# Layer norm's squares added on GpSimd before TensorE sums them, in a two-layer image kernel

## The chip, the cores and the metric

The kernel runs on one core of a Trainium2 chip. The metric is the device time of one execution in microseconds (us). The core's engines work side by side, each through its own queue and in the order of that queue: TensorE (PE in the profile, PEld for its weight loads), VectorE (DVE), ScalarE (ACT), GpSimd (POOL), and SyncE (SP), which here only issues DMAs.

## What is computed

Eight images of 384 channels and 64 x 64 pixels pass two residual layers. The first layer is a group norm, a layer norm over the channels, and attention in windows of 8 x 8 pixels: one half of the heads (branch 0) on plain windows, the other half (branch 1) on windows shifted by 4 pixels. The second is a group norm, a channel mixing, a filter in the frequencies of each 8 x 8 block, a 3 x 3 convolution of each channel, a gate and a second mixing. The change touches the variance of the layer norm alone:

```python
x = x + _L0_conv_ref(_gn(x), ...)          # layer 0
x = x + _L1_conv_ref(_gn(x), ...)          # layer 1

# in _L0_conv_ref
xt = x.reshape(b, c, h * w).transpose(0, 2, 1)
mu = xt.mean(-1, keepdims=True)
var = ((xt - mu) ** 2).mean(-1, keepdims=True)
xt = (xt - mu) / jnp.sqrt(var + EPS) * norm_g + norm_b
qkv = (xt @ qkv_w + qkv_b).reshape(b, h * w, 3, c).transpose(2, 0, 1, 3)
...
out = out @ proj_w + proj_b
```

## The kernel before

**Tiles.** An image is cut into 8 strips of 8 rows, 512 pixels each, so there are 64 strips. A strip is a tile of 128 partitions x 3 chunks of channels x 512 pixels in float32 (384 channels = 128 x 3), with the pixels put in the order of the windows.

**A strip's way through layer norm.** `group_normal` (L308, VectorE) writes the group-normed strip y. `ln_square` (L313, ScalarE) squares all three chunks into `sq`, of which there is one buffer. `ln_sums` (L317 on) lets TensorE sum y and `sq` over the channels: a matrix of ones scaled by 1/384, 32 columns wide, is the weight, and for each of the three chunks four matmuls of 128 pixels write to four groups of 32 rows of one PSUM bank (`ln`). These are 12 matmuls for y and 12 for `sq`; each float32 matmul is two records in the profile. ScalarE copies the sums out (`m`, L325), VectorE and ScalarE form one over the standard deviation (`lr`, L327 to L330), and two DMAs spread it over all partitions by way of DRAM (`line`, `rs`). `ln_scale` (L341, VectorE) multiplies y by it. The mean is not subtracted from y: the weights were centred for that.

**What follows.** `shifted_half` (L354 to L356, POOL) copies halves of two neighbouring strips into `y2` (and `yw`) for branch 1. `qk_tile` (pq) and `v_tile` (pvv) are the projections on TensorE, `scores` (pS), `weights` and `exponent` the softmax, `turn` (pT) and `apply` (pA) the weighted sum, `put` (po) and `project` (pr) the output. `v_tile` also has POOL set a column of ones in `v` (L397). In the second layer `mix` (pt), `transform` (pf), `back` (pz), the convolution (`conv`, L651, up to eight VectorE instructions a chunk, on the accumulator zz) and `finish` (pw on TensorE, the output sum x_finish on VectorE, L684) follow.

**The order.** All pieces are put in a list with a due place each and emitted sorted by it; a unit of place is half of a strip's share of time. The attention of one image runs beside the second layer of the image before it, so the first image has attention alone and the last second layer stands alone at the end. `ln_square` has its place at v + 0.45 and `ln_sums` at v + 0.99, where v is two strips ahead of the strip's attention. A scheduler may reorder what is emitted, but for the TensorE instructions, which keep the order of the program.

**The start.** Before the first attention the kernel reads the first image, takes its group statistics, and prepares the weights: `pack_qk` (L118) gathers the q and k columns on VectorE and POOL, and `qk_weights` and `v_weights` fold the norm's bias in (`pb`, `pv`) and centre the weights (`pc` on TensorE, then a subtraction on VectorE, L185). In TensorE's order the first strip's `ln_sums` stands ahead of all of this preparation, the second strip's behind the first `pc`. On POOL the 64 small DMAs of the position tables (`rpb_raw`, L154) and the memsets of the convolution's borders (L268, L269) come first, then POOL's part of `pack_qk`.

Of the kernel before, what the change touches and what calls it, by code (L numbers as in the profile page):

```python
# [9 lines left out]
ALU = mybir.AluOpType  # L10
AX = mybir.AxisListType

P = 128
KC = 3
# [18 lines left out]
def block_kernel(ctx: ExitStack, tc: tile.TileContext, out, x, consts, fsel, wqk, wv, bqk, bv,  # L33
                 wp, bp, lng, lnb, rpb1, rpb2, w_in, w_dw, w_out, filt):
    nc = tc.nc
# [8 lines left out]
    def psum(name):  # L44
        return ps.tile([P, ST], F32, tag="gemm", name=name)
# [6 lines left out]
    def matmul(*args, **kw):  # L52
        tc.keep_in_program_order(nc.tensor.matmul(*args, **kw))  # L53
# [4 lines left out]
    def strip(tag, bufs, name):  # L58
        return sb.tile([P, KC, ST], F32, tag=tag, bufs=bufs, name=name)

    def row512(tag, bufs, name):
        return sb.tile([P, ST], F32, tag=tag, bufs=bufs, name=name)
# [9 lines left out]
    for s in range(NS):  # L72
        tag, bufs = ("x", 5) if s < 5 else (("xn", 1), ("ow", 1), ("y2", 1))[s - 5]
        t = strip(tag, bufs, f"x_first{s}")
# [188 lines left out]
    xs, ys, y2s, qks, vs, os_, ots, x1s, zs = ({} for _ in range(9))  # L263
# [47 lines left out]
    def ln_square(b, s):  # L311
        sq = ys[b, s, "sq"] = strip("sq", 1, f"sq_{b}_{s}")
        nc.scalar.activation(sq, ys[b, s], AF.Square)  # L313

    def ln_sums(b, s):


        p = psum(f"ln_{b}_{s}")
        for to, t in ((0, ys[b, s]), (P, ys.pop((b, s, "sq")))):
            for k in range(KC):  # L320
                for j in range(4):
                    matmul(p[32 * j:32 * (j + 1), to:to + P], ones_c[:, 0:32], t[:, k, j * P:(j + 1) * P],
                           start=(k == 0), stop=(k == KC - 1))
        m = sb.tile([P, 2 * P], F32, tag="lc", bufs=1, name=f"m_{b}_{s}")
        nc.scalar.copy(m, p[:, 0:2 * P])  # L325
        rc = sb.tile([P, P], F32, tag="lr", bufs=2, name=f"lr_{b}_{s}")
        nc.vector.tensor_tensor(rc, m[:, 0:P], m[:, 0:P], ALU.mult)  # L327
        nc.vector.tensor_tensor(rc, m[:, P:2 * P], rc, ALU.subtract)
        nc.scalar.activation(rc, rc, AF.Sqrt, bias=eps_t)
        nc.vector.reciprocal(rc, rc)  # L330

        line = dr.tile([4, P], F32, tag="line", bufs=4, name=f"line_{b}_{s}")
        queue = nc.scalar if b == 0 and s < 2 else nc.sync
        queue.dma_start(out=line, in_=rc[0:P:32, :])
        rs = ys[b, s, "rs"] = row512("rs", 2, f"rs_{b}_{s}")
        queue.dma_start(out=rs, in_=bass.AP(line.tensor, line.offset, [[0, P], [1, ST]]))
# [354 lines left out]
    for b in range(B):  # L691
# [17 lines left out]
        for s in range(NS):  # L709
# [3 lines left out]
            at(v - 0.84, load, b, s, "norm")  # L713
            at(v + 0.15, group_normal, b, s)
            at(v + 0.45, ln_square, b, s)
            at(v + 0.99, ln_sums, b, s)
            at(v + 1.35, ln_scale, b, s)

# [163 lines left out]
```

## Time and profile before

| | |
|---|---|
| Time, median of 3 runs | 3784.95 us (3780.62 to 3785.55) |
| The profiled execution | 3783.99 us, of which span 3782.0 |
| TensorE busy | 3675.0 us (97%) |
| VectorE busy | 2819.9 us (75%) |
| ScalarE busy | 2379.1 us (63%) |
| GpSimd busy | 272.9 us (7%) |
| Sums of y (`ln<-y`), 1536 records | 56.6 us busy |
| Sums of squares (`ln<-sq`), 1536 records | 54.5 us busy |
| Squares (L313), 64 instructions | 95.1 us busy, 1486 ns each |

The span is the part of an execution that the trace covers, from its first instruction to its last. Busy time counts each moment once, however many records overlap in it; that is why 1536 matmuls of some 275 ns make 55 us. A share of busy time is an average over stages with different limits: what a change is worth is read from the stage it lies in, by what is waited for there. The profile names tiles without their numbers and lines by `kernel.py`; all matmuls are recorded at L53, all transposes at L56, so TensorE's work is told apart by the tile that it writes.

### The profile page before, as it was taken

To read this page: it belongs to the slowest core of one execution; us is meant where nothing else is said; L and a number is where in the kernel's file an instruction comes from. 1 tells how busy PE (TensorE), PEld (TensorE's weight loads), DVE (VectorE), ACT (ScalarE), POOL (GpSimd) and SP (SyncE) were. 2 spreads that over 40 slices of the span, in tenths; PEclk is the share of its full clock that TensorE was granted. 3 is DMA by queue.
4 is the path that set the end of the run, shared out by engine and by line. 5 is a ranking of instruction groups with operands and counts; after the bars stand their busy time and mean duration, and the time that the engine had idled before them with its cause. 6 is when DMAs were issued, how large, how long until landed. Compare 5 with 4: busy or idle time off the path is not lost.

```text
span 3782.0 us, 90249 instructions
## 1 busy us (share of the span) xinstructions
PE 3675.0 (97%) x39168; PEld 2347.3 (62%) x39168; DVE 2819.9 (75%) x4601; ACT 2379.1 (63%) x3946; POOL 272.9 (7%) x648
## 2 busy tenths in 40 slices
PE   6999999999999999999999999999999999999998
PEld 4666666666666666665666666666666666666554
DVE  5655578778878688777877778877788777777898
ACT  3766676656666576665766666666676666676442
POOL 4000000000000000000000000000000000000000
PEclk9999999999999999999999999999999999999999
DMA  4222223223322233223332322322232222222422
GB/s 121 88 96 85 89 85 111 82 87 123 117 91 104 74 120 119 103 80 115 115 104 93 109 91 99 132 79 107 93 119 99 107 88 82 98 79 74 157 101 76
DMA packets 144496, 377.16 MB, mean 100 GB/s; under 512 B 12308, under 2 KB 12900, under 8 KB 144100
## 3 DMA queue, kind: packets, MB, share of 16 engines
q1 hardware_dynamic: 139952, 370.60, 27.8%
q8 instruction: 308, 5.05, 0.6%
q0 software_dynamic: 2048, 0.15, 0.1%
q10 hardware_dynamic: 2100, 0.63, 0.1%
q14 instruction: 88, 0.72, 0.1%
HBM read 270.54 MB, written 100.79 MB: 98 GB/s over the span
## 4 chain that ended last, share of the span: by engine, by line
PE 87%; DVE 5%; ACT 4%; DMA 2%; issue 2%; SPq 0%; ACTq 0%; DVEq 0%
PE pq L53 24%; PE pt L53 13%; PE pr L53 13%; PE pvv L53 12%; PE pw L53 7%; PE pS L53 3%; PE pA L53 3%; PE pz L53 3%; PE pT L56 3%; PE po L56 3%; PE ln L53 2%; DVE zz L651 2%; PE pf L53 2%; PE pc L53 1%; DMA rs<-line 1%
## 5 line engine op out<-in xcount | busy, mean ns | idle before, releaser
L651 DVE SCALAR_TENSOR_TENSOR zz<-z,dw_sb,zz 128x512 f32<-128x512 f32 x1490 | 1089.9, 750 | 192.6 <-ACT zz L645 169.7
L53 PE MATMUL pq<-y,wqk_sb 128*128 128x512 f32 x2160 | 990.1, 596 | 0.0
L53 PEld LDWEIGHTS pq<-y,wqk_sb 128*128 128x128 f32 x2160 | 402.8, 190 | 456.2 <-issue 423.3
L53 PE MATMUL pt<-wi_sb,xn 128*128 128x384 f32 x1536 | 535.2, 487 | 1.4 <-DVE x_finish L684 1.4
L53 PE MATMUL pr<-oT,wp_sb 128*128 128x512 f32 x1152 | 523.1, 593 | 1.0 <-DVE oT L515 1.0
L53 PE MATMUL pvv<-wv_sb,y 128*128 128x192 f32 x2880 | 495.9, 326 | 0.0
L53 PEld LDWEIGHTS pvv<-wv_sb,y 128*128 128x128 f32 x2880 | 471.7, 190 | 36.2 <-issue 23.0
L372 ACT ACTIVATE qab<-pq,bq_sb,cst 96x512 f32<-96x512 f32 (+1 forms) x256 | 197.8, 773 | 400.0 <-PE pq L53 398.3
L53 PEld LDWEIGHTS pt<-wi_sb,xn 128*128 128x128 f32 x1536 | 286.2, 190 | 206.8 <-issue 48.0
L372 ACT ACTIVATE kcd<-pq,vec 32x512 f32<-32x512 f32 x512 | 348.4, 680 | 9.0
L53 PEld LDWEIGHTS pr<-oT,wp_sb 128*128 128x128 f32 x1152 | 211.2, 190 | 224.3 <-issue 211.8
L327 DVE TENSOR_TENSOR lr<-m 128x128 f32<-128x128 f32 x64 | 18.7, 292 | 355.4 <-ACT m L325 355.4
L645 ACT ACTIVATE zz<-z,dw_sb 128x512 f32<-128x512 f32 x183 | 133.9, 733 | 199.8 <-PE pw L53 195.2
L372 ACT ACTIVATE qcd<-pq,bq_sb,cst 96x512 f32<-96x512 f32 (+1 forms) x256 | 197.0, 769 | 43.9 <-PE pq L53 40.6
L524 DVE SCALAR_TENSOR_TENSOR x_add<-pr,vec,x_add 128x512 f32<-128x512 f32 x192 | 143.5, 747 | 108.5 <-PE pr L53 106.5
L354 POOL COPY y<-y 128x384 f32<-128x384 f32 x112 | 99.7, 890 | 1719.7 <-PE pvv L53 1217.1
L562 ACT COPY t<-pt 128x384 f32<-128x384 f32 x256 | 124.7, 487 | 157.4 <-PE pt L53 154.3
L406 ACT COPY v<-pvv 128x384 f32<-128x384 f32 x256 | 121.6, 479 | 142.2 <-PE pvv L53 141.5
L53 PE MATMUL pw<-zz,wo_sb 128*128 128x512 f32 x384 | 182.9, 613 | 0.0
L372 ACT ACTIVATE kab<-pq,vec 96x512 f32<-96x512 f32 (+1 forms) x256 | 174.1, 680 | 8.8 <-PE pq L53 7.1
L56 PEld LDWEIGHTS pT<-cst,e 128*128 128x128 f32 x1024 | 119.3, 141 | 66.9 <-issue 40.1
L441 DVE TENSOR_TENSOR e<-e,mx 128x1024 f32<-128x1024 f32 x128 | 158.0, 1234 | 2.5
(138 smaller groups left out, 5194.9 us busy)
## 6 DMA issues: line engine op xcount, KB each, us to landing
x_add<-in_x_dram SPq DMA_DIRECT2D x64, 768.0 KB, 9.4
x1d<-x_add SPq DMA_DIRECT2D x64, 768.0 KB, 5.4
x_mix<-x1d SPq DMA_DIRECT2D x64, 768.0 KB, 4.3
x_finish<-x1d SPq DMA_DIRECT2D x64, 768.0 KB, 6.4
out_dram<-x_finish SPq DMA_DIRECT2D x64, 768.0 KB, 3.8
x_norm<-in_x_dram SPq DMA_DIRECT2D x61, 768.0 KB, 7.7
x_stats<-in_x_dram SPq DMA_DIRECT2D x56, 768.0 KB, 8.0
rs<-line SPq DMA_DIRECT2D x62, 256.0 KB, 3.3
```

Of the source, the lines that this page charges most:

```text
L53: tc.keep_in_program_order(nc.tensor.matmul(*args, **kw))
L56: tc.keep_in_program_order(nc.tensor.transpose(*args, **kw))
L327: nc.vector.tensor_tensor(rc, m[:, 0:P], m[:, 0:P], ALU.mult)
L354: nc.gpsimd.tensor_copy(dst[:, :, :, :, 0:4], src[:, :, :, :, 4:8])
L372: return nc.scalar.activation(dst[to:to + n], pq[of:of + n], AF.Identity, bias=bias[of:of + n], scale=scale)
L406: nc.scalar.copy(v[:, 2 * g:2 * g + 2, :, 0:HD], pvv[:, 0:384].rearrange("p (g h d) -> p g h d", g=2, h=4))
L441: zs["soft"] = nc.vector.tensor_tensor(e, e, mx.unsqueeze(2).to_broadcast([P, 2 * NS, 64]), ALU.subtract)
L524: nc.vector.scalar_tensor_tensor(t[:, m, :], pr, bp_sb[:, m:m + 1], t[:, m, :], ALU.add, ALU.add)
L562: nc.scalar.copy(t1, pt[:, 0:C])
L645: nc.scalar.activation(zz.rearrange("p (r c) -> p r c", c=SW), z[:, 1:9, 1:SW + 1], AF.Copy, scale=dw_sb[:, m, 4:5])
L651: i = nc.vector.scalar_tensor_tensor(acc.rearrange("p (r c) -> p r c", c=SW), z[:, dy:dy + 8, dx:dx + SW], dw_sb[:, m, TAPS[tap]:TAPS[tap] ...
```

## The change

`ln_square` gets two additions on GpSimd, in place: the second and then the third chunk of the squares are added to the first. `ln_sums` sums the three chunks of y as before, but of the squares the first chunk alone. The title under which the change was made also names residuals ahead of the softmax; the code that it means (a dependency called "residual first") is in both kernels, and the diff has nothing of it.

```diff
     def ln_square(b, s):
         sq = ys[b, s, "sq"] = strip("sq", 1, f"sq_{b}_{s}")
         nc.scalar.activation(sq, ys[b, s], AF.Square)
+        for k in (1, 2):
+            nc.gpsimd.tensor_tensor(sq[:, 0, :], sq[:, 0, :], sq[:, k, :], ALU.add)
 
     def ln_sums(b, s):
 
 
         p = psum(f"ln_{b}_{s}")
-        for to, t in ((0, ys[b, s]), (P, ys.pop((b, s, "sq")))):
-            for k in range(KC):
+        for to, t, n in ((0, ys[b, s], KC), (P, ys.pop((b, s, "sq")), 1)):
+            for k in range(n):
                 for j in range(4):
                     matmul(p[32 * j:32 * (j + 1), to:to + P], ones_c[:, 0:32], t[:, k, j * P:(j + 1) * P],
-                           start=(k == 0), stop=(k == KC - 1))
+                           start=(k == 0), stop=(k == n - 1))
```

## The prediction

> **What bounds the kernel now.** I read the page first: the shares of busy time, then the chain that ended last. Its lines give span or busy microseconds with the share of the span.
>
> ```profile
> PE 3675.0 (97%) x39168; PEld 2347.3 (62%) x39168; DVE 2819.9 (75%) x4601; ACT 2379.1 (63%) x3946; POOL 272.9 (7%) x648
> PE 87%; DVE 5%; ACT 4%; DMA 2%; issue 2%; SPq 0%; ACTq 0%; DVEq 0%
> ```
>
> TensorE holds the chain for 87% and is busy 97%. Cut into stretches, it is busy 26.1 of the first 61 us and 3313.5 of the 3359 us from 61 to 3420, where all other layer norms lie: there it is idle 45 us, in pieces of at most 2.7 us. So in that long stretch a microsecond taken from TensorE is a microsecond off the end. The first 61 us are another regime: a serial chain. The second look was therefore the timeline around one layer norm (start, duration, engine, line, operands):
>
> ```profile
> 581.12 1.48 ACT L313 ACTIVATE sq<-y 128x1536 f32<-128x1536 f32 x1 [2.06 <-DVE y L308]
> 583.56 0.12 POOL L397 MEMSET v<- 128x16 f32 x1 [15.94 <-ACT z L607]
> 610.64 0.86 PE L53 MATMUL ln<-y,cst 128*32 128x128 f32 x24
> 611.32 0.84 PE L53 MATMUL ln<-sq,cst 128*32 128x128 f32 x24
> 612.08 0.88 PE L53 MATMUL pf<-t,cst 64*64 64x192 f32 x16
> ```
>
> Twelve matmuls show as 24 records (two for each float32 matmul). The 24 sums of y occupy TensorE from 610.64 to 611.32, 0.68 us, 28.3 ns a record: four column groups run side by side, so the 273 ns of one record is not its price. The square is finished at 582.60, and TensorE wants it 28.7 us later. Over the 64 strips that slack is 14 to 45 us, but for the first two, where it is 0.05 and 1.74 us. So the third look was the chain and POOL's timeline at the start:
>
> ```profile
> 34.55 1.49 ACT sq L313
> 36.09 1.51 PE ln L53 x24
> 37.60 3.93 PE pb L53 x18
> 41.53 4.05 PE pc L53 x6
> 60.94 7.72 PE pq L53 x18
> ...
> 40.95 5.81 POOL L154 DMA_DIRECT2D rpb_raw<-in_rpb_dram  x10 [0.46 <-DMA rpb_raw<-in_rpb_dram]
> 47.22 0.49 POOL L269 MEMSET z<- 128x10 f32 x1
> 47.26 2.00 POOL L118 COPY wqk_sb<-wqk_raw 128x48 f32<-128x48 f32 x6
> ```
>
> From 36.09 TensorE goes through the weight preparation with 1.5 us of idle time to the first pq at 60.94. The first sum of squares stands at the head of that run. POOL meanwhile issues 64 small DMAs one by one until 46.8, and clears borders until 47.5.
>
> **What the Trainium skill says.** Three places bear on this.
> - "GPSIMD Engine Reference", section Elementwise — side-by-side cycle accounting: a two-input add of 2048 float32 a partition takes 4497 ns; a quarter of that is 1.12 us for 512. No run before shows such an add; POOL's one-input copy of 384 takes 0.50 us alone, 0.67 us for 512 if scaled.
> - The same page, section Instruction dispatch: the first call of a freshly loaded GpSimd library pays about 6 us more, with no instruction to show for it. No run here shows it.
> - "SBUF — State Buffer", section Who interferes with whom: a VectorE instruction with two SBUF inputs and a GpSimd instruction that reads SBUF exclude each other for a whole instruction. The trace agrees in kind: the 0.50 us copy L354 takes 1.43 where it meets a subtraction with two SBUF inputs, and the 0.74 us convolution tap behind it takes 0.99.
>
> ```profile
> 565.01 1.22 DVE L441 TENSOR_TENSOR e<-e,mx 128x1024 f32<-128x1024 f32 x1
> 565.15 1.43 POOL L354 COPY y<-y 128x384 f32<-128x384 f32 x1 [7.85 <-DVE y L341]
> 566.14 0.99 DVE L651 SCALAR_TENSOR_TENSOR zz<-z,dw_sb,zz 128x512 f32<-128x512 f32 x1
> ```
>
> **The change part by part.** The built order of instructions shows what the diff alone does not. On TensorE 512 matmuls (8 a strip) are gone and the rest stands as it was. POOL has 128 adds more and, ahead of the first add, one instruction that loads a GpSimd library. VectorE and ScalarE are reordered in the first 60 us only; the SP queue and its DMAs are the same. That the change doesn't do what it says is thus excluded.
>
> *TensorE.* 16 records fewer a strip, at 28.3 ns: 0.453 us. Times 62 strips with slack: **-28.1 us**. If the whole interval of the group (611.32 to 612.08, 0.76 us) shrank in proportion, it were 0.51 us and 31.6; if the last matmul's tail or the next group's inputs ate a little, 0.40 and 25. The first two strips run at 63 and some 41 ns a record: another -1.65, taken with the start.
>
> *The adds in the long stretch.* Two adds, the second waiting for the first, take about 2.4 us against 14 us of slack or more, and from the third strip on POOL's previous instruction ended at least 0.3 us before the square did: TensorE doesn't wait for them. Behind them in POOL's queue stand the memset of v's column of ones (0 to 9 us after the square; read by pA, a phase later) and the copies of the shifted rows, which wait for pvv 20 us on. These cost nothing; if the cover went, pA would be late next, by at most 2.4 us. ScalarE's next square waits for TensorE's read of the single sq buffer, as now.
>
> *VectorE against the adds.* I laid each strip's 2.5 us after the square over VectorE's instructions with two SBUF inputs. They overlap by 26 us in all, in most strips by 0 to 0.25. The exceptions are the fifth strip of each later image (seven, 1.4 to 2.1 us) and the fourth of five of them (1.1 to 1.9), beside two strips at the start. At the fifth, a pair of taps at +1.16 us leads over the output sums to TensorE's pt, which waits for them already:
>
> ```profile
> 932.53 1.54 DVE L651 SCALAR_TENSOR_TENSOR zz<-z,dw_sb,zz 128x512 f32<-128x512 f32 x2 [1.95 <-ACT zz L645]
> 937.41 1.88 DVE L684 TENSOR_TENSOR x_finish<-pw,x_finish 128x512 f32<-128x512 f32 x3
> ```
>
> A pair of 1.12 us adds there holds the taps up by some 1.25 us, of which about 0.6 us of hand-over may hide a half: 0.7 us times 7 images, **+5 us**. Bounds: 0 (a lock can only delay, and VectorE is idle some 23% of the stretch around it), and 15 (1.25 us at all twelve).
>
> *The start.* The first adds stand in POOL's queue behind the 64 DMA issues, the memsets and the library load, and two weight copies stand between them. Borders done 47.5; load 6 (estimate by the skill); add 1.2; two copies 0.7 (their 0.47 and 0.26); add 1.2: 56.6. TensorE's sum of squares starts then and not at 36.1: 20.5 us late, and the whole weight preparation with it, since TensorE takes its queue in order. Less 1.65 for the shorter sums: **+18.9 us** at the first pq, which no idle time behind it takes up (337.5 of 339 us busy from 61 to 400). What else moves there has room. The third strip's adds and the shifted copies behind them on POOL, and on VectorE the second strip's scaling, which now stands ahead of the centring of the second branch's weights, come out at about 86 by the same durations; the second branch's pq, 12.7 us behind the first, needs them at 92. Bounds: no load time and adds of 0.7 give +12; a load of 14 and adds of 2 give +28. Nothing excludes the upper side; a gain is excluded, for POOL is busy until 47.5.
>
> **Sum.** -28.1 + 18.9 + 5 = -4.2. The profiled execution took 3783.99 (span 3782.0 and 2 around it), 1 under the median of 3784.95. 3784.0 - 4.2 gives **3780**.
>
> **The rivals.**
> - *Faster* (chance 0.32): the load costs nothing that shows and VectorE's delays are absorbed. The start then costs 47.5 + 3.1 - 36.1 - 1.65 = 12.9, and -28.1 + 12.9 gives 3769. For it: VectorE idles 0.5 to 2 us after most squares. Against: a library load is in the instructions.
> - *Slower* (0.22): the load in the start takes 20 us, as a fetch from HBM that nothing covers. -28.1 + 32.9 + 5 = +9.8: 3794. It decides from a load of 18 us up. For it: TensorE's whole queue hangs on it. Against: the skill's price is a third of that.
> - *Slower by VectorE* (0.06): the lock is lost in every strip. 2.4 us times 62 is 149; if a sixth of it reached TensorE, +25, and 3784 - 28 + 19 + 25 = 3800. For it: the 1.43 and 0.99 above. Against: 26 us of overlap in all.
>
> **How the numbers follow.** Gain and start nearly cancel in the likeliest case (0.40): within 0.2% (7.6 us, about what a measurement of this kernel can tell from no change), its own range 3776 to 3790. Faster by more 0.32, slower by more 0.28. All low bounds together give 3784 - 31.6 + 12 = 3764, all high ones 3784 - 25 + 28 + 15 = 3802; 3766 to 3797 leaves out the outermost and the lost lock.
>
> **What would show it.** Right: the records of y's sums still 1536, those of sq's 512; from the first pq to the last layer norm the stretch shorter by 23 us (28 less 5); the first sum of squares near 56 to 57 and pq near 80; adds near 1.1 us. Wrong: a first pq before 72 or after 90 (the load), a wait of TensorE for the adds beyond the first two strips, or pt's waits for x_finish grown by over 2 us an image.

## The result, and the profile after

| | before | after |
|---|---|---|
| Time, median of 13 runs | 3783.06 us | 3774.86 us |
| Ratio, 95% interval | | 0.9977 (0.9969 to 0.9986) |
| Profiled execution, its span | 3782.0 us | 3771.3 us |
| First pq of the first image | 60.8 us | 78.3 us |
| Copy of the third strip's sums (m) | 90.8 us | 108.3 us |
| Copy of the last strip's sums (m) | 3404.0 us | 3394.8 us |

The change makes the kernel faster by 0.23% (0.14 to 0.31), 8.7 us. The forecast was 4.2 us, to 3780, and its range of 3766 to 3797 holds the result. Behind the small sum stand two large terms, as forecast: 17.5 us are lost before the first pq, and 26.7 us come back between the third and the last layer norm (3404.0 - 90.8 = 3313.2 us before, 3394.8 - 108.3 = 3286.5 after).

The page of the kernel after: busy time and instructions of each engine, the chain by engine, and the group of the new adds.

```profile
PE 3639.9 (97%) x38144; PEld 2315.5 (61%) x38144; DVE 2839.3 (75%) x4601; ACT 2379.7 (63%) x3946; POOL 438.2 (12%) x776
PE 86%; DVE 5%; ACT 4%; issue 2%; DMA 2%; POOL 0%; ACTq 0%; DVEq 0%; POOLq 0%
L315 POOL TENSOR_TENSOR sq<-sq 128x512 f32<-128x512 f32 x128 | 167.4, 1308 | 634.3 <-ACT sq L313 629.3
```

TensorE has 1024 records fewer and is busy 35 us less, POOL 165 us more, and the chain is still TensorE's. VectorE runs the same 4601 instructions, but they take 19 us more; in the kernel without the adds (below) they take 2819.9 us as before, so it is the adds that lengthen them. An add takes 1.27 us in the median and 1.31 in the mean; the estimate worked out from the Trainium skill's "GPSIMD Engine Reference", section Elementwise — side-by-side cycle accounting, was 1.12.

The timeline of the kernel after around the same strip as in the prediction (start, duration, engine, line, operands):

```profile
594.52 1.49 ACT L313 ACTIVATE sq<-y 128x1536 f32<-128x1536 f32 x1 [2.44 <-DVE y L308]
596.09 2.63 POOL L315 TENSOR_TENSOR sq<-sq 128x512 f32<-128x512 f32 x2 [15.13 <-ACT sq L313]
598.65 0.13 POOL L399 MEMSET v<- 128x16 f32 x1
623.31 0.86 PE L53 MATMUL ln<-y,cst 128*32 128x128 f32 x24
623.99 0.40 PE L53 MATMUL ln<-sq,cst 128*32 128x128 f32 x8
624.33 0.88 PE L53 MATMUL pf<-t,cst 64*64 64x192 f32 x16
```

The adds follow 0.1 us behind the square, are done at 598.7, and TensorE comes for their sum 25 us later. From the first sum of y to pf it now takes 1.02 us instead of 1.44. Over the 62 strips from the third on, the mean from the first sum to TensorE's next group is 1.011 us instead of 1.447: 0.436 us a strip.

The start of the kernel after, in the chain of waits (start, duration, what):

```profile
41.20 6.63 POOL rpb_raw L154 x12
...
48.44 0.03 POOLq L315
48.47 1.30 POOL sq L315
49.78 0.36 POOL wqk_sb L118 x2
50.13 1.23 POOL sq L315
51.36 0.04 issue
51.40 0.66 PE ln L53 x8
52.06 3.93 PE pb L53 x18
...
64.45 1.23 DVE lr L330
65.68 1.42 DVE wv_sb L181
67.10 0.04 issue
67.14 2.93 PE pc L53 x4
70.07 3.65 PE pb L53 x18
```

The chain of the start, which ran over the image's load and TensorE before, runs over POOL's table DMAs now. The library load that the prediction counted on shows only as two records in POOL's queue (MODIFY_POOL_CONFIG, taken here to be the load) at 48.29 and 48.32, 0.15 us each; in the timeline the add begins at 48.39, behind the last memset. TensorE comes to its sum of squares at 51.4, 15.3 us later than before.

### The profile page after: what moved, and what is told of

It reads as the page before. It is cut to its first block, busy times and chain, and to the rows that moved or that the text cites. A ratio compares the mean times of both kernels' runs of the same rounds, so it can differ in the third digit from the quotient of the medians.

```text
span 3771.3 us, 88216 instructions
## 1 busy us (share of the span) xinstructions
PE 3639.9 (97%) x38144; PEld 2315.5 (61%) x38144; DVE 2839.3 (75%) x4601; ACT 2379.7 (63%) x3946; POOL 438.2 (12%) x776
## 4 chain that ended last, share of the span: by engine, by line
PE 86%; DVE 5%; ACT 4%; issue 2%; DMA 2%; POOL 0%; ACTq 0%; DVEq 0%; POOLq 0%
PE pq L53 24%; PE pr L53 13%; PE pt L53 13%; PE pvv L53 12%; PE pw L53 6%; PE pS L53 3%; PE pA L53 3%; PE pz L53 3%; PE pT L56 3%; PE po L56 3%; DVE zz L653 2%; PE pf L53 2%; PE ln L53 2%; PE pc L53 1%; DMA rs<-line 1%
## 5 line engine op out<-in xcount | busy, mean ns | idle before, releaser
L653 DVE SCALAR_TENSOR_TENSOR zz<-z,dw_sb,zz 128x512 f32<-128x512 f32 x1490 | 1106.5, 761 | 189.3 <-ACT zz L647 166.5
L315 POOL TENSOR_TENSOR sq<-sq 128x512 f32<-128x512 f32 x128 | 167.4, 1308 | 634.3 <-ACT sq L313 629.3
L449 ACT ACTIVATE e<-e 128x1024 f32<-128x1024 f32 x128 | 135.3, 1057 | 53.4 <-DVE e L443 52.0
```

The source lines that it names most:

```text
L315: nc.gpsimd.tensor_tensor(sq[:, 0, :], sq[:, 0, :], sq[:, k, :], ALU.add)
L449: nc.scalar.activation(e, e, AF.Exp)
L653: i = nc.vector.scalar_tensor_tensor(acc.rearrange("p (r c) -> p r c", c=SW), z[:, dy:dy + 8, dx:dx + SW], dw_sb[:, m, TAPS[tap]:TAPS[tap] ...
```

## The experiments

All ratios are to the kernel before, which ran beside each of these kernels; "us off" and "us on" are that ratio times its median. The median itself differed between three sessions (3782.4 to 3788.4 us), so kernels are compared by ratio. What is read from a trace is one execution of each kernel.

**The start as before.** In the first three strips neither adds nor shorter sums:

```diff
-        for k in (1, 2):
+        for k in (1, 2) if (b or s > 2) else ():
...
-        for to, t, n in ((0, ys[b, s], KC), (P, ys.pop((b, s, "sq")), 1)):
+        for to, t, n in ((0, ys[b, s], KC), (P, ys.pop((b, s, "sq")), 1 if (b or s > 2) else KC)):
```

> The changed kernel, but the first three strips keep three chunks of squares on TensorE and no adds. Theory (the start pays 17.6 us because the first add stands behind POOL's 64 DMA issues; 0.44 us a strip is gained afterwards): the first pq is back at about 61 us, and 61 strips times 0.44 leave 3783 - 27 = 3756. Rival (the start's loss lies elsewhere, or the steady gain is smaller and the start only looks late): within 5 us of the changed kernel, 3770 to 3780. Rival (a library load of 6 us): it shows between the first square with adds and its first add, in the fourth strip, and costs nothing there.

Measured: 3755.7, ratio 0.9924 (0.9910 to 0.9937), 28.8 us off (24 to 34). This is the theory's number, and 20 us better than the kernel after. The first pq is at 58.5. Six of the kernels in this section leave the start as before, and theirs lies at 58.5 to 61.7, so some 3 us are scatter between executions. The first add of this kernel, on POOL's timeline, behind a square that ends at 110.41:

```profile
110.50 2.61 POOL L315 TENSOR_TENSOR sq<-sq 128x512 f32<-128x512 f32 x2 [7.07 <-ACT sq L313]
```

It starts 0.09 us later. That does not price the load: its records stand at 103.38, and POOL was idle for 7.07 us ahead of the add, so 6 us of loading could have passed unseen.

**The start alone.** The complement: the conditions above turned to `b == 0 and s < 3`.

> The complement: adds and one-chunk sums in the first three strips alone. Theory: first pq at 78 to 79 us, and the loss stays to the end: 3783 + 17 = 3800. Rival (the later stages take the late start up, since DMAs and weights are ready by then): 3783 to 3790.

Measured: 3798.9, ratio 1.0040 (1.0026 to 1.0053), 15 us on (10 to 20), first pq at 76.8. Nothing behind takes the late start up. The two halves, -28.8 and +15.1, add up to -13.7; the whole gave -8.7 (-5.3 to -11.7), which the intervals of the two halves allow.

**The tables' DMAs on SP.** The adds stay everywhere:

```diff
-                nc.gpsimd.dma_start(
+                nc.sync.dma_start(
                     out=raw[half, h // 2, y2 * WS:(y2 + 1) * WS],
```

> The changed kernel with the 64 small DMAs of the position tables issued by SP instead of POOL. Theory (POOL's queue makes the adds late): the first add starts within 1 us of the first square, about 3 us of adds stay in the chain, first pq at 62 to 65, total 3783 - 27 + 2 = 3758. Rival (the library load): the first add comes 6 us after the square, first pq near 70, 3764. Rival (neither): as the changed kernel, 3775. A loss to SP's own queue would show as loads that come late after 100 us.

Measured: 3759.8, ratio 0.9934 (0.9920 to 0.9947), first pq at 59.7. The first adds on POOL's timeline, and TensorE behind them:

```profile
33.11 2.74 POOL L315 TENSOR_TENSOR sq<-sq 128x512 f32<-128x512 f32 x2 [1.97 <-ACT sq L313]
35.91 0.65 PE L53 MATMUL ln<-sq,cst 128*32 128x128 f32 x8 [3.68 <-POOL sq L315]
```

POOL is idle ahead of the adds and TensorE waits 3.7 us instead of 14.7. So it is the place behind 64 DMA issues that cost most of the start. Of 6 us for a load nothing shows: its records stand at 31.09, and the first add starts 2.0 us behind them, as soon as the square is done. The adds are not free: the 3.7 us are theirs. An earlier image hides most of them here (the first square starts at 31.55 instead of 34.55); this helps the first pq, which comes even before the expected 62 to 65. Of loads that come late nothing shows either: between the third and the last layer norm TensorE is idle for 50.3 us here and for 50.6 in the kernel after.

**No adds.**

```diff
-        for k in (1, 2):
-            nc.gpsimd.tensor_tensor(sq[:, 0, :], sq[:, 0, :], sq[:, k, :], ALU.add)
```

> The changed kernel without the adds: two thirds of the squares are left out of the variance; TensorE's work is that of the changed kernel. It prices TensorE's gain alone, with no POOL instruction to wait for or to block VectorE. Theory: 62 strips times 0.453 and 1.65 at the start, 3783 - 29.7 = 3753; the kernel with the start as before is above it by the start's 1.65 and by what VectorE loses to the adds. If the lock costs 5 us as forecast, the two differ by 6 to 7 us; if it costs nothing in the sum, by 2.

Measured: 3758.0, ratio 0.9927 (0.9914 to 0.9939): no better than the kernel with the start as before, against the expectation. The total doesn't answer the question, since this kernel's VectorE order at the start is another and its first pq comes at 63.6, 5.1 us after the other's. The stretch between the third and the last copy of the sums does: 3282.1 us here, 3287.0 with the adds. TensorE is busy there for 3236.9 us here and 3237.1 with the adds, so the whole difference is idle time, 45.2 against 49.9 us; pt's waits for x_finish are 1.6 us here and 6.5 there. So the adds cost some 5 us. That is one execution each; the same stretch of code took 3313.2 us before and 3315.8 with the start alone, so 2 to 3 us are scatter.

**The adds alone.** From the fourth strip on the adds run, and TensorE sums three chunks all the same.

> From the fourth strip on the adds, but TensorE goes on to sum three chunks (the first then holds the sum already, so squares are counted twice): the cost of the adds with none of the gain, the start as before. Theory (they delay VectorE's taps only at the fifth strip of an image, where TensorE's pt waits for the output sums): pt's waits for x_finish go from 1.4 to 6 or 7 us, total 3783 + 5 = 3788. Rival (the lock costs something at every strip): 61 times 0.3 us or more, over 3800. Rival (the adds cost nothing): 3783 to 3785, pt's waits unchanged.

Measured: 3790.6, ratio 1.0005 (0.9999 to 1.0012), 2 us on (-0.4 to 4.5). TensorE's waits (total, times, longest):

```profile
PE pt L53 <- DVE x_finish L686: 6.9, 6, 1.4
```

The waits are the forecast ones: six, one at the fifth strip of each image from the third to the eighth, where the kernel before has four of at most 0.5 us. They are 5.5 us more in all. The time alone doesn't show them: it is below the forecast 5 us and would fit adds that cost nothing. The rival of a cost at each strip, 18 us or more, is excluded.

**y summed on GpSimd too.**

```diff
+        if b or s > 2:
+            y = ys[b, s]
+            nc.gpsimd.tensor_tensor(sq[:, 1, :], y[:, 0, :], y[:, 1, :], ALU.add)
+            nc.gpsimd.tensor_tensor(sq[:, 1, :], sq[:, 1, :], y[:, 2, :], ALU.add)
```

> The start as before; from the fourth strip on GpSimd adds the three chunks of y as well, into the second chunk of the squares' tile, and TensorE sums one chunk of each: 4 + 4 matmuls in place of 12 + 4. Theory (a record of TensorE is worth 28.3 ns wherever the square has slack): 61 times another 0.453 is 27.6 below the kernel with the start as before, 3728, plus up to 6 for twice the time on the port shared with VectorE: 3728 to 3734. Rival (TensorE's next inputs become late once the sums shrink to 0.5 us, or VectorE falls behind): 3740 to 3756.

Measured: 3766.6, ratio 0.9944 (0.9932 to 0.9957), 21 us off (16 to 26). The theory fails, and the rival, which names VectorE falling behind as its cause, falls short too: from 3783 this ratio is 3762, above its 3740 to 3756. TensorE is busy 24.6 us less than with the squares alone (3620.7 against 3645.3) and idle 28.0 us more (140.0 of its span against 112.0). 17.4 us of that are waits of pt for x_finish; the rest is spread over many small waits. pt's waits in this kernel, then the adds of y (duration in ns, smallest, median, largest):

```profile
PE pt L53 <- DVE x_finish L692: 23.9, 21, 2.2
```

```profile
L318 POOL TENSOR_TENSOR sq<-y x61: 1262/1297/2241, 110.0 to 3355.0; 128x512 f32<-128x512 f32 x61
L319 POOL TENSOR_TENSOR sq<-sq,y x61: 1267/1596/2135, 111.4 to 3356.3; 128x512 f32<-128x512 f32 x61
```

Four adds last over 5 us. In the third, fifth, sixth and seventh strip of the later images (but for the last one's sixth and seventh) VectorE's taps begin 1.2 to 2.7 us after the square already in the kernel before, so there they meet adds. pt waits 21 times instead of 6, and 20 of these waits lie in those four strips.

**The adds on VectorE.** As with the start as before, with `nc.vector` in place of `nc.gpsimd`.

> The start as before; the adds of the other 61 strips on VectorE instead of GpSimd. 122 adds of about 0.68 us are 83 us more on an engine busy for 75%. Theory (TensorE has the chain, and VectorE's own queue is late only at a few strips): the gain of 27 stays but for about as much as the lock took or a little more, 3756 to 3765. Rival (VectorE becomes the bound of the later images): 3775 or more.

Measured: 3761.7, ratio 0.9932 (0.9919 to 0.9946). 122 adds of 0.69 us are 84 us on an engine that was busy for 75%, and pt waits for x_finish 2.6 us. VectorE as the bound of the later images, at 3775 or more, is excluded. From GpSimd's 0.9924 this can't be told apart: what gains is TensorE's shorter sum, not the engine that adds.

**Adds only where VectorE idles.** `one` says where the squares are added, `y1` where y is:

```diff
+        one = s != 4 if b else s > 2
+        y1 = s in (0, 1, 3, 7) if b else s > 2
```

> Adds placed by what VectorE does after the square. As with the start as before, but from the second image on the fifth strip keeps three chunks on TensorE, and y is added on GpSimd too in 33 strips: the fourth to eighth of the first image, and of the later ones the first, second, fourth and eighth, where VectorE's next tap comes 3.5 us or more after the square or pt did not wait. Theory (adds cost where they meet the taps ahead of x_finish, in the third, fifth, sixth and seventh strips, and nothing else): pt's waits for x_finish stay at 1 to 4 us, and 33 times 0.453 = 15 us come off beside the 2 us of the fifth strips: ratio to before about 0.988, 3738 to 3742. Rival (twice the adds cost as such, wherever they stand): no better than the kernel with the start as before, 0.992 or more.

> As with the start as before, and from the second image on the fifth strip keeps three chunks of squares on TensorE, without adds. Theory (the whole loss to the shared port sits at the fifth strips): pt's waits for x_finish fall from 6.5 to 1 or 2 us, 7 times 0.453 = 3.2 us of gain are given up, 2 us net: ratio about 0.992, at the edge of what can be told. Rival (the waits stand elsewhere too): pt's waits stay above 4 us and the time is 1 to 3 us above that of the kernel with the start as before.

Measured: with y in 33 strips 3753.5, ratio 0.9923 (0.9910 to 0.9937); with the fifth strip as before alone 3757.3, ratio 0.9932 (0.9918 to 0.9945). pt's waits are as the theory has them with y in 33 strips, and near its 1 to 2 us in the other kernel. These waits in the kernel with y in 33 strips, then in that with the fifth strip as before:

```profile
PE pt L53 <- DVE x_finish L693: 3.2, 7, 0.5
```

```profile
PE pt L53 <- DVE x_finish L686: 2.4, 6, 0.5
```

So the fifth strip holds most of what was lost to the adds (6.5 us of waits fall to 2.4), and adds placed clear of the taps make pt wait hardly more. The time is less plain. TensorE's busy time differs by 16.3 us, the profiled spans by 12 (3746.8 against 3758.7), but of these executions one is the fastest of its four and the other the slowest of its five; the ratios differ by only 0.0009, each of them good to 0.0014. By the time the first theory fails (0.9923, not 0.988) and its rival's number came, though the waits speak against the rival's reason. The 15 us of gain are thus not shown in the runs, nor is the forecast 2 us of the fifth strip; what takes the rest stays open. The start as before (0.9924), these two, the tables on SP and the adds on VectorE (0.9923 to 0.9934) beat both kernels and can't be told apart: the start as before is the simplest.

## Why the prediction was right

**TensorE's gain: right, a little large.** 16 records at 28.3 ns were to be 0.453 us a strip. The group went from 1.447 to 1.011 us, 0.436 a strip; times 62 that is 27.0, not 28.1. With y summed on GpSimd too, another 16 records fewer take it to 0.574, 0.437 less again. So a record costs 27.3 ns, and 0.14 us of the group don't shrink with their number; the 28.3 ns had a part of these in it.

**The stretch behind the start: right, not to the microsecond.** Forecast 23 us shorter from the first pq to the last layer norm; by the trace it is 26.7 between the copies, and by the ratio 8.7 + 17.5 = 26. Counted from each record to the next, the sums of these 61 strips take 26.6 us less and TensorE is idle 5.2 us more, which makes 21. The rest is in groups that the change doesn't touch: pw takes 4.1 us less and pS 2.0. In the start alone, whose code here is that of the kernel before, pw takes 3.4 us less too, so this may be scatter; it is not explained. The terms as measured (-27.0, +17.5 and +5.8 for pt's waits, below) add up to -3.7, near the forecast -4.2, and the runs gave -8.7 (-5.3 to -11.7): the 5 us between them stay open.

**VectorE against the adds: right in place, near in size.** The fifth strip of the third image in the kernel after, on POOL, VectorE and TensorE:

```profile
939.22 2.96 POOL L315 TENSOR_TENSOR sq<-sq 128x512 f32<-128x512 f32 x2 [12.50 <-ACT sq L313]
940.31 2.43 DVE L653 SCALAR_TENSOR_TENSOR zz<-z,dw_sb,zz 128x512 f32<-128x512 f32 x2 [1.95 <-ACT zz L647]
946.08 1.88 DVE L686 TENSOR_TENSOR x_finish<-pw,x_finish 128x512 f32<-128x512 f32 x3
946.82 2.20 PE L53 MATMUL pt<-wi_sb,xn 128*128 128x384 f32 x6 [1.35 <-DVE x_finish L686]
```

The pair of taps takes 2.43 us instead of 1.54, and the pair of adds 2.96 instead of 2.63: each side holds the other up, as the Trainium skill's "SBUF — State Buffer", section Who interferes with whom, states. The taps come 0.9 us later by this, where 1.25 was forecast. pt waits 1.35 us where it waited 0.31. Over all, these waits went from 1.4 to 7.2 us, in six images and not seven, where +5 was forecast.

**The start: the sum near, its working wrong, and luck in between.** Forecast +18.9 at the first pq, measured +17.5 (and +16.0 with the start alone). The library load, 6 us by the Trainium skill's "GPSIMD Engine Reference", section Instruction dispatch, took nothing that shows: the adds ended at 51.4 and not at 56.6. The shorter sums of the first two strips saved 1.2 us and not 1.65 (in the chain, 0.85 and 0.32). By these two alone the first pq would have come at 60.9 + 15.3 - 1.2 = 75.1. The other 3.5 us arose behind the wait, where the forecast took the old durations over and held that what else moves has room. That one error of 6 us met others that filled more than half of it is luck.

1.3 of the 3.5 us arose at the v weights, and there it is the adds again. POOL and VectorE in the kernel after, then VectorE in the kernel before:

```profile
64.27 2.60 POOL L315 TENSOR_TENSOR sq<-sq 128x512 f32<-128x512 f32 x2 [7.55 <-ACT sq L313]
64.42 1.26 DVE L330 TENSOR_TENSOR lr<-m,lr 128x128 f32<-128x128 f32 x1
```

```profile
49.99 0.28 DVE L328 TENSOR_TENSOR lr<-m,lr 128x128 f32<-128x128 f32 x1
```

The third strip's pair of adds runs beside VectorE's work on the second strip's lr and on the v weights. The subtraction into lr takes 1.26 us instead of 0.28 and ends 0.15 us behind the first add; the scaling of wv_sb behind it (L181) takes 1.49 instead of 0.41 and ends 0.22 us behind the second. TensorE's pc waits 2.0 us for it instead of 0.9. In the start alone and with the tables on SP, which have these adds, the same two take 1.3 and 1.49 us; with the start as before and without adds they take 0.3 and 0.4. The prediction had seen an overlap at two strips of the start and left it out of its sum.

The remaining 2.2 us are TensorE's own: the second pb took 3.65 us instead of 1.92 for the same 18 records, and the first and the last pc took 0.14 and 0.30 longer. TensorE's granted clock was low there. Windows of the kernel after, of the kernel before and of that with the tables on SP (stretch, its length, busy time and instructions of PE, PEld, DVE, ACT and POOL, then the clock):

```profile
64.00:80.00 16.00, 13.27 (x35) 8.55 (x35) 11.79 (x19) 0.59 (x2) 5.72 (x11) 0.57 0.08 24
```

```profile
48.00:62.00 14.00, 12.46 (x56) 8.33 (x57) 8.56 (x18) 2.17 (x3) 3.72 (x15) 0.76 0.07 24
```

```profile
48.00:64.00 16.00, 14.01 (x38) 7.82 (x39) 12.21 (x20) 1.06 (x3) 5.72 (x11) 0.69 0.13 26
```

The kernel before has such a stretch too; in the kernel after it is deeper, and the second pb falls into it at a clock of 0.50 (68 to 76 us). That the idle 15 us are the cause is not shown: with the tables on SP TensorE waited 3.7 us for the adds and was granted 0.69, and it had 0.50 from 48 to 52.

**The rivals.** *Faster, with a load that costs nothing* gave 3769. It had its first premise right and its second wrong: VectorE's delays were not absorbed, neither at pt (5.8 us) nor at the start (1.3). *Slower by the load* is excluded: in the kernel after and in the start alone the first add begins 0.1 us behind the load's records, and with the tables on SP 2.0 us behind them. *Slower by VectorE in every strip* is excluded by the adds alone. The likeliest case gave 3780 and its own range 3776 to 3790; the runs lie at 3774.9, just past it and just past 0.2%. Of the signs of being right, the record counts, the shorter stretch and the first pq came; the first sum of squares came at 51.4 and not at 56 to 57, and an add took 1.27 us and not 1.1.

## What to carry to other kernels

When an engine with much idle time takes over work, look for what stands ahead of it in that engine's queue at each place, not at its share of busy time: POOL was 7% busy, and the adds of three strips out of 64, run alone, cost 15.1 us where those of the other 61 gained 28.8. Exempting the few instances that lie in the serial start was worth 20 us here; none of the tunings of the steady part that were tried added to it in the runs. Where two engines hold each other up, ask which of the slower one's instructions fall on a stretch that leads to the bound engine: the same adds made TensorE's pt wait up to 1.4 us at the fifth strip of six images and not at all at the other strips.

## What the runs showed that was not expected

- Loading a GpSimd library ahead of the first add cost nothing visible in two places of the stream: the add began 0.1 us behind the load's records at 48.3 (kernel after; the start alone shows the same) and 2.0 us behind those at 31.09 (tables on SP).
- Doubling the work on GpSimd from two to four adds a strip took 24.6 us from TensorE's busy time, and the time did not fall (0.9944 against 0.9924): pt's waits rose from 6.5 to 23.9 us, nearly all of them in strips where VectorE's taps begin within 2.7 us of the square.
- A GpSimd add held up not only a VectorE instruction that reads two tiles (lr, 1.26 us instead of 0.28) but also a scaling that reads one tile and a vector (wv_sb, L181, 1.49 instead of 0.41).
- Each of these four starts had a stretch of low granted clock: 0.76 from 48 to 62 us before, 0.57 from 64 to 80 after, 0.57 from 62 to 78 in the start alone, 0.69 from 48 to 64 with the tables on SP. What sets its depth stays open.
